# Later steps for layer 1's norms and for image 1's features, and another buffer for image 1's run weights, in a four-layer image kernel

## The chip, the cores and the metric

The kernel runs on one core of a Trainium2 chip. The metric is the device time of one execution in microseconds (us); three executions give a median. The engines are PE (TensorE, matrix products), ACT (ScalarE), DVE (VectorE), POOL (GpSimd) and SP (SyncE, which here issues DMAs).

## The reference

Four images of 64 x 64 pixels and 64 channels, float32, pass through four layers.

- Layer 0 is attention over the 4,096 pixels of an image: q, k and v are linear maps of x, and the result is `gamma * softmax(q k^T) v + x`, with a small gamma.
- Layer 1 has two halves. First: a layer norm over the channels, a pointwise map to 256 channels, a 3 x 3 depthwise convolution, the product of the two halves of the channels (a gate), a scale for each channel from the mean over all pixels (`sca`), a pointwise map to 64 channels, and `x + beta * ...`. Second: a layer norm, a pointwise map to 256, the gate, a pointwise map back to 64, and `x + gamma * ...`.
- Layer 2 is attention of the image with itself, `softmax(x x^T) x` over the pixels. Its scores are symmetric.
- Layer 3 is a non-local block with maps g, phi, theta of 32 channels, a softmax over the pixels, an output map, a batch norm over the whole batch, and a residual.

## The kernel before, in words

Everything of an image is kept in SBUF: `X[:, b]` is image b as 128 partitions (64 channels, two halves of the pixels) x 2,048 columns. Attention runs by items. An item computes a block of scores on PE into a slot of PSUM, ACT turns it into exponentials e with row sums, and PE multiplies e with the values two or so items later, into accumulator banks. PSUM is one tile PS: slots of 1,024 columns are handed out in turn by `new_ps` (two while layer 0 runs, three once image 3's last layer-0 product is out), and banks 6 and 7 accumulate.

**The order is written out by hand.** A list `items` holds layer 0 of images 0 to 3 (32 items each), then layer 2 of image 0 (100 items; I call the n-th score step of that layer row n), then layer 2 of image b with layer 3 of image b - 1, and so on. Beside it run two lanes of Python generators: `conv` (layer 1, added at item 32b + 34, so that layer 1 of image 3 begins with layer 2 of image 0) and `misc` (loads, projections, `features2`, and others). Each item advances the lanes by some nominal microseconds, and a generator's `yield us` says how far its next piece lies behind. The numbers in the yields are distances in that count, not times of the chip. The instruction order of PE, ACT, DVE and POOL is the order of recording; the order of SP's DMA queue is left to the scheduler.

**norm (L1159 to L1191)**, used twice in layer 1 of each image. Two Squares of x on ACT (L1164); after the first yield the sums on PE (L1170: four matmuls on x, four on the squares, which sum over the channels by the constant `jsel`); the variance (L1175 on ACT, L1176 on DVE); Ln and Exp on ACT (L1178, L1179); eight DMAs on SP that broadcast the result to all partitions (L1183); after a yield of 11.0 two multiplications by x on DVE (L1191).

**layer1 (L1194 to L1297).** The first norm writes y; pointwise products L1205; ACT writes them into the padded image `pad` (L1222); nine taps for each of 4 x 2 blocks (L1236 on ACT for image 3, L1240 on DVE), the gate with its sums on DVE (L1251), their total `ytot` (L1257), then the small product with `sca` on PE (L1260) and the scaled weights pw2s on DVE (L1262, L1264), and the products with them (L1269) and the residual (L1274 on ACT, L1276 on DVE). The second norm writes z; then for each of four blocks two products L1205, ACT's t (L1288), DVE's u (L1290), a product L1294 and a residual (L1295, L1297).

**features2 (L1301 to L1314)** makes the keys `ko` of layer 2 for an image: four transposes on PE (L1309), each followed by a copy on DVE and one on ACT (L1312) and a DMA on SP for each (L1313).

**Layer 2.** Scores L1387, exponentials L1392, products L1448. Because scores are symmetric, some blocks of e are used a second time, mirrored: DVE transposes them (L1405, tile `turned`), and a run of 64 small matmuls (L1473) multiplies them with the run weights `xr`, a regrouped copy of the image that 16 DMAs for each h make on SP (L1364). A run's result and an accumulator's are added to `A` by DVE (L1486, L1488, L1462; an accumulator of image 0 partly by a copy on ACT, L1459).

**Layer 0 around it.** Scores L1095, exponentials L1100, products L1121; the last products of an image are added to X, quarter by quarter, with gamma (L1133).

**Buffers that matter.** The pool "xn" has one buffer: y, z, xr of images 1 to 3, and a DMA sum of layer 3 live in it one after another. The pool "pad" has one: the padded image, and later `wy` of images 0 and 1 (layer 3's output before its batch norm). xr of image 0 has a buffer of another pool. A tile that takes over a buffer waits for the last reader of the one before.

Lines of this text and of the profile are those of the kernel before; in the changed kernel those behind L1356 are three higher.

Of the kernel before, what the change touches and what calls it, by code (L numbers as in the profile page):

```python
# [8 lines left out]
F32 = mybir.dt.float32  # L9
# [682 lines left out]
def fast_path(ctx: ExitStack, tc: tile.TileContext, a: dict, out: bass.AP, bad):  # L692
    nc = tc.nc
    B, H, W, C = a["x"].shape
# [9 lines left out]
    xn = ctx.enter_context(tc.tile_pool(name="xn", bufs=1))  # L704
# [21 lines left out]
    def new_ps():  # L726
        if turn_of["banks"]:
            if turn_of["bank"] % turn_of["banks"] == turn_of["banks"] - 1:
                turn_of["bank"] += 1
            k = new_bank(), new_bank()  # L730
            return PS[:, 512 * k[0] : 512 * k[0] + 1024]
        s = turn_of["slots"][turn_of["ps"] % len(turn_of["slots"])]
        turn_of["ps"] += 1
        return PS[:, bass.ts(s, 1024)]

    def piece():
        if turn_of["banks"]:
            return PS[:, bass.ts(new_bank(), 512)]
        return new_ps()[:, 0:512]
# [8 lines left out]
    def new_e(name="e"):  # L748
        return ep.tile([128, 2048], F32, tag="e", name=name)

    def new_t(name="t"):
        return tp.tile([128, 1024], F32, tag="t", name=name)

    def new_big(name):
        return big.tile([128, 4096], F32, tag="big", name=name)

    def new_pad(name="pad"):
        return big.tile([128, 66 * PW + 2], F32, tag="pad", name=name, bufs=1)
# [233 lines left out]
    def at(i, fn):  # L992
        due.setdefault(i, []).append(fn)
# [162 lines left out]
            items.append((lambda t=t: item(t), 0.0))  # L1156


    def norm(x, y):  # L1159


        sq = [new_t("sq"), new_t("sq")]
        for i in range(2):
            act(sq[i], x[:, bass.ts(i, 1024)], AF.Square)  # L1164
        yield 4.5
        ps = new_ps()
        for i, src in enumerate(((x, x), (sq[0], sq[1]))):
            for j in range(4):
                c = 512 * j if i == 0 else 512 * (j % 2)
                mm(  # L1170
                    ps[32 * j : 32 * j + 32, bass.ts(i, 512)], jsel, src[j // 2][:, c : c + 512],
                    start=True, stop=True,
                )
        t = new_t()
        act(t[:, 0:512], ps[:, 0:512], AF.Square)  # L1175
        stt(t[:, 0:512], t[:, 0:512], -1.0, ps[:, 512:1024], ALU.mult, ALU.add)  # L1176
        yield 4.0
        act(t[:, 0:512], t[:, 0:512], AF.Ln, bias=eps1)  # L1178
        act(t[:, 512:1024], t[:, 0:512], AF.Exp, scale=-0.5)  # L1179
        yield 3.0  # L1180
        for j in range(4):
            for h in range(2):
                nc.sync.dma_start(  # L1183
                    out=y[64 * h : 64 * h + 64, bass.ts(j, 512)],
                    in_=t[32 * j + 16 * h : 32 * j + 16 * h + 16, 512:1024]
                    .unsqueeze(1).to_broadcast([16, 4, 512]),
                )
        yield 11.0
        for jp in range(2):
            cols = bass.ts(jp, 1024)  # L1190
            nc.vector.tensor_mul(y[:, cols], y[:, cols], x[:, cols])  # L1191
            yield 1.8
# [6 lines left out]
    def layer1(b):  # L1199
        x = X[:, b]  # L1200
# [8 lines left out]
                    )  # L1209

        y = xn.tile([128, 2048], F32, tag="xn", name="xn")
        yield from norm(x, y)
        yg = new_big("yg")
        yw = yg.rearrange("c (s q p h) -> c p q s h", s=2, p=2, h=H)
        ysum = sm.tile([128, 8], F32, tag="ysum", name="ysum")
# [39 lines left out]
                    yield 1.8  # L1255
        ytot = sm.tile([128, 1], F32, tag="ytot", name="ytot")
        nc.vector.tensor_reduce(ytot, ysum, AX.X, ALU.add)  # L1257
        yield 12.0 if b == B - 1 else 7.0
        ps = new_ps()
        mm(ps[:, 0:1], sca, ytot, start=True, stop=True)  # L1260
        ch = sm.tile([128, 1], F32, tag="ch", name="ch")
# [15 lines left out]
            yield 3.0  # L1277
        z = xn.tile([128, 2048], F32, tag="xn", name="xn")
        far = 1.2 if b == B - 1 else 1.0
        for us in norm(x, z):  # L1280
            yield far * us
        for j in range(4):
            t, u = new_t(), new_t("u")
# [18 lines left out]
    def features2(b):  # L1302
        x = X[:, b]
        im[b].ko = ko = new_big("ko")
        kv = ko[:, 0:N].rearrange("p (a e n) -> p a e n", e=2, n=128)
        for g in range(4):
            ps = piece()
            for i in range(4):
                nc.tensor.transpose(ps[:, bass.ts(i, 128)], x[:, bass.ts(4 * g + i, 128)], ident)  # L1309
            for e, copy in enumerate((nc.vector.tensor_copy, nc.scalar.copy)):  # L1310
                own, other = slice(64 * e, 64 * e + 64), slice(64 - 64 * e, 128 - 64 * e)
                copy(kv[own, bass.ts(g, 4), e, :], ps[own, :].rearrange("p (a n) -> p a n", n=128))  # L1312
                nc.sync.dma_start(out=kv[other, bass.ts(g, 4), e, :], in_=kv[own, bass.ts(g, 4), e, :])  # L1313
            yield 3.5  # L1314

    SIDES = [[(7, (h + 1) % 7), ((h + 2) % 7, (h + 3) % 7)] for h in range(7)]
    FULL = [(7, [7])] + [(h, [h] + SIDES[h]) for h in range(6)] + [(6, SIDES[6] + [6])]
# [6 lines left out]
    def layer2(b, when_free=None):  # L1324


        x, m, first = X[:, b], im[b], len(items)
# [20 lines left out]
        st = {"e": {}, "T": {}, "esum": {}}  # L1348
# [8 lines left out]

        def weights(h):
            if "xr" not in st:
                st["xr"] = new_e("xr") if b == 0 else xn.tile([128, 2048], F32, tag="xn", name="xn")  # L1360
            for q in range(4):
                for k in range(4):
                    c = 1024 * (h % 2) + 256 * k
                    nc.sync.dma_start(  # L1364
                        out=st["xr"][32 * q : 32 * q + 32, c : c + 256],
                        in_=x[32 * k : 32 * k + 32, 256 * h : 256 * h + 256],
                    )
# [157 lines left out]
    def close2(b):  # L1525
        x, m = X[:, b], im[b]
        ps, tot, n = piece(), sums2[:, b, :], 4 * max(m.mirrored) + 4
        cs = m.cs.rearrange("p (j k) -> p j k", k=4)
        for k in range(4):
            mm(ps[32 * k : 32 * k + 32, 0:n], sel4, cs[:, 0:n, k], start=True, stop=True)  # L1530
        g = 0
        while g < 8:
            k = g
            while k < 8 and m.count[k] == m.count[g]:
                k += 1
            nc.vector.tensor_reduce(
                tot[:, 4 * g : 4 * k],
                m.zs[:, m.first[g] : m.first[g] + 4 * m.count[g] * (k - g)]
                .rearrange("p (t k) -> p t k", k=m.count[g]), AX.X, ALU.add,
            )  # L1540
            g = k
        nc.vector.tensor_add(tot[:, 0:n], ps[:, 0:n], tot[:, 0:n])
        rz = sm.tile([128, 32], F32, tag="rz2", name="rz2")
        nc.vector.reciprocal(rz, tot)
        yield
        for i in range(4):
            ps = new_ps()
            for j in range(8):
                c = 1024 * i + 128 * j
                nc.tensor.transpose(ps[:, bass.ts(j, 128)], m.A[:, c : c + 128], ident)  # L1550
            blocks_ = ps.rearrange("p (j n) -> p j n", n=128)
            nc.vector.tensor_mul(
                blocks_, blocks_, rz[:, bass.ts(i, 8)].unsqueeze(2).to_broadcast([128, 8, 128])
            )
            xs = x[:, bass.ts(i, 512)].rearrange("p (j h) -> p j h", h=H)
            for o in range(2):
                nc.vector.tensor_add(xs, ps.rearrange("p (j o h) -> p j o h", j=8, o=2)[:, :, o, :], xs)  # L1557
            yield
# [48 lines left out]
    def keys3(b):  # L1607
        m = im[b]
        m.ph = new_big("ph")
        keys = m.ph.rearrange("p (s n) -> p s n", s=2)  # L1610
        for j in range(4):
            for k in range(4):
                nc.sync.dma_start(
                    out=keys[32 * k : 32 * k + 32, :, bass.ts(j, 512)],
                    in_=m.own[32 * j : 32 * j + 32, :, :],
                )
# [185 lines left out]
    conv_from, misc_from, misc_to = {}, {}, {}  # L1802
    for b in range(B):
# [3 lines left out]
        if b + 1 < B:  # L1807
            gens = [load_x(i) for i in range(1, B)] if b == 0 else []
            misc_from[32 * b + 16] = gens + [project0(b + 1)]
        conv_from[32 * b + 34] = layer1(b)  # L1810
    misc_from[112] = [features2(0)]
    for b in range(B):
        misc_to[len(items)] = True
        f = len(items)
        if b == 0:
            layer2(b)
            misc_from[f + 82] = [features2(b + 1)]
        else:
            layer2(b, lambda b=b: keys3(b - 1))
            turns = close2(b - 1)  # L1820
            for i in (10, 13, 22, 32, 42) if b == 1 else (8, 12, 22, 32, 42):
                at(f + i, lambda turns=turns: next(turns))
            misc_from[f + 46] = [open3(b - 1)]
            f = len(items)
            misc_to[f] = True
            layer3(b - 1)
            if b + 1 < B:
                turns = features2(b + 1)
                for i in (4, 7, 10, 13):
                    between3[f + i] = 2, lambda turns=turns: next(turns)  # L1830
    f = len(items)
# [220 lines left out]
```

## Time and profile before

| | |
|---|---|
| median of three executions | 2459.12 us (2457.01, 2459.12, 2463.22) |
| profiled execution, whole | 2458.65 us |
| its span, first to last instruction | 2456.9 us |
| mean granted clock of PE | 0.997 |
| PE busy, idle in the span | 2412.4 us, 44.5 us |
| DVE, ACT, POOL busy | 1467.3, 1651.4, 533.0 us |
| layer 1 of image 3, from its first sums to the last residual | about 1025 to 1280 us |
| layer 2 of image 0 in PE's order | from about 1017 us on |

How to read it: a line of the timeline is the start, the duration, the engine, the source line, the operation, the tile written and those read, the shapes and how many instructions are run together; in brackets stands the idle time before and what ended it. A line of the waits is the waiting engine, tile and line, what it waited for, and then the sum in us, how often, and the longest. In a table of windows each engine has its busy time and its count, and the last three numbers are the granted clock as a share of full speed, the DMA engines' share, and GB/s.

### The profile page before, as it was taken

Reading aid. Unit: us, or ns where it says so; the run is one execution under the profiler, and the core shown is the slowest. Engines: PE = TensorE matmul, PEld = TensorE weight load, DVE = VectorE, ACT = ScalarE, POOL = GpSimd, SP = SyncE. Lnnn points to the kernel's source line nnn. Section 1 sums busy time; section 2 is a strip of 40 time slices with the busy share of each in tenths; the row PEclk is TensorE's granted clock in tenths of the full one; section 3 lists DMA queues with packets and bytes.
Section 4 is the critical chain, followed back from the end, with each engine's and each line's share of the span. In section 5 each row is a group of like instructions: output and inputs, shape, how many; then the busy total and the mean of one; then the engine's idle time right before and its main releaser. Section 6 shows DMA issues by size and latency. Waiting matters only on the chain.

```text
span 2456.9 us, 63395 instructions
## 1 busy us (share of the span) xinstructions
PE 2412.4 (98%) x27381; PEld 927.5 (38%) x27381; DVE 1467.3 (60%) x1784; ACT 1651.4 (67%) x3144; POOL 533.0 (22%) x383
## 2 busy tenths in 40 slices
PE   9999999999999999999899999999999999999998
PEld 3343453336433633344334442144431344421113
DVE  2010377227822773278656668876668866678886
ACT  4666766676666666668654459954479744579996
POOL 2000000000000000010136551255631365622110
PEclk9999999999999999999999999999999999999999
DMA  3000000000000000250530026610075300286554
GB/s 80 1 18 1 19 1 18 18 19 1 18 18 18 2 19 18 55 119 2 123 81 23 19 66 134 139 27 23 16 151 118 78 20 20 71 170 141 120 117 117
DMA packets 67668, 136.39 MB, mean 56 GB/s; under 512 B 13004, under 2 KB 34229, under 8 KB 67381
## 3 DMA queue, kind: packets, MB, share of 16 engines
q0 software_dynamic: 24320, 86.55, 17.4%
q1 hardware_dynamic: 42309, 43.85, 7.8%
q8 instruction: 217, 3.56, 0.6%
q10 hardware_dynamic: 752, 1.85, 0.2%
q14 instruction: 70, 0.57, 0.1%
HBM read 4.80 MB, written 4.19 MB: 4 GB/s over the span
## 4 chain that ended last, share of the span: by engine, by line
PE 85%; DVE 8%; ACT 4%; issue 1%; SPq 1%; DMA 0%; DVEq 0%; ACTq 0%
PE PS L1121 18%; PE PS L1095 18%; PE PS L1448 9%; PE PS L1387 9%; PE PS L1635 9%; PE PS L1696 8%; PE PS L1473 7%; DVE tg L1687 2%; PE PS L1205 2%; ACT e L1646 2%; DVE y L1240 2%; ACT e L1100 1%; PE PS L1170 1%; ACT e L1392 1%; DVE X L1557 1%
## 5 line engine op out<-in xcount | busy, mean ns | idle before, releaser
L1100 ACT ACTIVATE e<-PS 128x1024 f32<-128x1024 f32 x512 | 524.2, 1024 | 331.3 <-PE PS L1095 298.4
L1392 ACT ACTIVATE e<-PS 128x512 f32<-128x512 f32 x632 | 371.5, 595 | 350.6 <-PE PS L1387 329.9
L1121 PE MATMUL PS<-e,vq 64*64 64x512 f32 x4096 | 577.3, 592 | 0.0
L1095 PE MATMUL PS<-X,q 64*64 64x512 f32 x4096 | 574.5, 590 | 1.8 <-DVE X L979 1.7
L1646 ACT ACTIVATE e<-PS 128x512 f32<-128x512 f32 (+2 forms) x588 | 500.2, 921 | 59.3 <-PE PS L1635 38.6
L1687 DVE TENSOR_TENSOR tg<-tg,e 128x2048 f32<-128x2048 f32 x172 | 393.8, 2290 | 42.8 <-ACT e L1646 31.4
L1387 PE MATMUL PS<-ko 64*64 64x512 f32 x2528 | 346.3, 596 | 1.3 <-DVE A L1488 0.7
L1448 PE MATMUL PS<-e,X 64*64 64x512 f32 x2528 | 340.7, 593 | 1.4 <-ACT own L1459 0.8
L1240 DVE SCALAR_TENSOR_TENSOR y<-pad,vec,y 128x1024 f32<-128x1024 f32 x240 | 307.9, 1283 | 14.3 <-ACT y L1236 7.0
L1427 POOL TENSOR_TENSOR esum<-esum,e 128x1024 f32<-128x1024 f32 x126 | 299.3, 2376 | 49.0 <-ACT e L1392 42.0
L1405 DVE STREAM_TRANSPOSE turned<-e 128x1024 f32<-128x1024 f32 x196 | 240.9, 1238 | 107.5 <-ACT e L1392 107.5
L1635 PE MATMUL PS<-tg,ph 32*64 32x512 f32 x4096 | 294.9, 612 | 1.7 <-ACT e L1646 0.8
L1095 PEld LDWEIGHTS PS<-X,q 64*64 64x64 f32 x4096 | 184.1, 133 | 258.8 <-issue 178.4
L1121 PEld LDWEIGHTS PS<-e,vq 64*64 64x64 f32 x4096 | 184.2, 133 | 251.9 <-issue 158.6
L1421 POOL DMA_DIRECT2D esum<-e x28 | 22.0, 786 | 1178.1 <-ACT e L1392 1081.5
L1696 PE MATMUL PS<-e,tg 128*32 128x512 f32 x2048 | 272.5, 604 | 0.0
L1108 DVE TENSOR_REDUCE sums<-zs 128x1 f32<-128x4 f32 x128 | 19.6, 153 | 260.0 <-ACT e L1100 259.8
L1448 PEld LDWEIGHTS PS<-e,X 64*64 64x64 f32 x2528 | 104.1, 133 | 171.8 <-issue 146.7
L1473 PE MATMUL PS<-turned,xn 32*64 32x256 f32 x5376 | 163.2, 377 | 4.0 <-DVE X L1557 3.5
L1668 POOL DMA_DIRECT2D xn<-e x116 | 101.3, 903 | 293.9 <-ACT e L1646 201.0
L1387 PEld LDWEIGHTS PS<-ko 64*64 64x64 f32 x2528 | 96.4, 133 | 164.2 <-issue 135.4
L1635 PEld LDWEIGHTS PS<-tg,ph 32*64 32x64 f32 x4096 | 63.4, 129 | 222.7 <-ACT e L1646 190.2
(218 smaller groups left out, 1677.8 us busy)
## 6 DMA issues: line engine op xcount, KB each, us to landing
xn<-e POOLq DMA_DIRECT2D x132, 512.0 KB, 5.2
esum<-e POOLq DMA_DIRECT2D x28, 512.0 KB, 4.7
xn<-X SPq DMA_DIRECT2D x336, 32.0 KB
xn<-t SPq DMA_DIRECT2D x64, 128.0 KB
ph<-tg SPq DMA_DIRECT2D x64, 128.0 KB
ko<-ko SPq DMA_DIRECT2D x32, 128.0 KB
xr<-in_x_dram SPq DMA_DIRECT2D x13, 256.0 KB
q<-q SPq DMA_DIRECT2D x12, 256.0 KB
```

Source lines behind the costliest of these rows:

```text
L1095: mm(ps[64 * c : 64 * c + 64, bass.ts(r, 512)], m.q[rows_, 128 * t + 64 * c : 128 * t + 64 * c + 64], x[rows_, bass.ts(g, 512)], start=Tru ...
L1100: act(es[g // 2][:, bass.ts(g % 2, 1024)], ps, AF.Exp, bias=SHIFT0, accum_out=zs[:, g : g + 1],)
L1121: ins = mm(PS[64 * s : 64 * s + 64, 2048 + 512 * j : 2560 + 512 * j], vq[rows_, :], es[j // 2][rows_, k : k + 512], start=t == 0 and i < 2 ...
L1240: stt(y1, win, wt, y1, ALU.mult, ALU.add)
L1387: mm(ps[64 * c : 64 * c + 64, bass.ts(r, 512)], m.ko[rows_, k : k + 64], m.ko[rows_, bass.ts(h, 512)], start=True, stop=True,)
L1392: act(e[:, bass.ts(r, 512)], ps[:, bass.ts(r, 512)], AF.Exp, bias=SHIFT2, accum_out=slot(g, 2 * u + r),)
L1448: mm(st["acc"][r][64 * c : 64 * c + 64, :], xw[rows_, 4 * g + 2 * u + c, :], st["e"][n][rows_, bass.ts(c, 512)], start=n == mine[h][0], st ...
L1473: mm(slots[q // 2][64 * c : 64 * c + 64, o : o + 256], st["xr"][rows_, w : w + 64], T[rows_, bass.ts(e, 256)], start=e < 2, stop=e >= 14,)
L1635: mm(PS[64 * c : 64 * c + 64, bass.ts(banks[k], 512)], m.ph[32 * k : 32 * k + 32, 128 * mc + 64 * c : 128 * mc + 64 * c + 64], m.th[32 * k ...
L1646: act(e[:, 512 * lo : 512 * k], PS[:, 512 * banks[lo] : 512 * banks[lo] + 512 * (k - lo)], AF.Exp,)
L1687: nc.vector.tensor_add(esum, esum, e)
L1696: mm(st["y"][32 * k : 32 * k + 32, :], m.gx[:, i % 32, :], es[i][:, bass.ts(k, 512)], start=mc == 0, stop=i % 32 == 31,)
```

## The change

Three things. The pieces of the norms are recorded somewhat later: the first yield of `norm` is 5.5 in place of 4.5 (both norms, all images), and for image 3 alone the yield before the multiplications is 2.0 longer in the first norm and 4.0 x 1.2 in the second, and that behind `ytot` is 14 in place of 12. `features2` of image 1 is recorded from item 89 of layer 2 of image 0 in place of 82, with its four pieces 3.0 apart in place of 3.5 (the 3.0 and 3.5 are the same code for images 0 and 1; image 2 and 3 call it from elsewhere, item by item). The run weights xr of image 1 live in the pad's buffer.

```diff
-    def norm(x, y):
+    def norm(x, y, more):
...
             act(sq[i], x[:, bass.ts(i, 1024)], AF.Square)
-        yield 4.5
+        yield 5.5
         ps = new_ps()
...
-        yield 11.0
+        yield 11.0 + more
         for jp in range(2):
             cols = bass.ts(jp, 1024)
             nc.vector.tensor_mul(y[:, cols], y[:, cols], x[:, cols])
...
-        yield from norm(x, y)
+        yield from norm(x, y, 2.0 if b == B - 1 else 0.0)
...
         nc.vector.tensor_reduce(ytot, ysum, AX.X, ALU.add)
-        yield 12.0 if b == B - 1 else 7.0
+        yield 14.0 if b == B - 1 else 7.0
...
-        for us in norm(x, z):
+        for us in norm(x, z, 4.0 if b == B - 1 else 0.0):
             yield far * us
...
-            yield 3.5
+            yield 3.0
...
-                st["xr"] = new_e("xr") if b == 0 else xn.tile([128, 2048], F32, tag="xn", name="xn")
+                st["xr"] = (
+                    new_e("xr") if b == 0 else new_pad("xr") if b == 1
+                    else xn.tile([128, 2048], F32, tag="xn", name="xn")
+                )
...
-            misc_from[f + 82] = [features2(b + 1)]
+            misc_from[f + 89] = [features2(b + 1)]
```

## The prediction

> **What bounds the kernel now.** I read the page's totals first, then the chain that ended last, the waits of TensorE (PE), and then the timeline around each wait, together with the granted clock.
>
> ```profile
> span 2456.9 us, 63395 instructions
> ...
> PE 2412.4 (98%) x27381; PEld 927.5 (38%) x27381; DVE 1467.3 (60%) x1784; ACT 1651.4 (67%) x3144; POOL 533.0 (22%) x383
> ...
> PE 85%; DVE 8%; ACT 4%; issue 1%; SPq 1%; DMA 0%; DVEq 0%; ACTq 0%
> ```
>
> PE is busy 98% and carries 85% of the chain. The change adds and removes no matmul, so it can only move PE's idle time (44.5 us) and whatever slows PE down. PE's waits, largest first:
>
> ```profile
> PE PS L1205 <- issue: 4.4, 1, 4.4
> ...
> PE PS L1170 <- ACT e L1100: 2.1, 3, 0.7
> ...
> PE PS L1260 <- DVE ytot L1257: 1.8, 1, 1.8
> PE PS L1205 <- ACT e L1392: 1.7, 1, 1.7
> ...
> PE PS L1309 <- ACT ko L1312: 0.9, 1, 0.9
> ```
>
> Columns: total us, times, longest. All five lie in lines that the change reschedules. Matmuls are pipelined, so a group's duration overlaps the next: a group shown as x8 costs 0.86 from start to start. I take a gap from there, not from the bracket. The 4.4 stands for 4.57 (the last group would end at 1222.57, the next starts at 1227.14), the first-norm 1.7 for 2.76, the 1.8 for 1.94.
>
> Three places in the timeline, with the releaser in brackets:
>
> ```profile
> 269.58 1.70 PE L1170 MATMUL PS<-sq,jsel 128*32 128x512 f32 x8
> ...
> 450.21 1.06 PE L1170 MATMUL PS<-X,jsel 128*32 128x512 f32 x8 [0.69 <-ACT e L1100]
> ...
> 447.16 1.99 ACT L1164 ACTIVATE sq<-X 128x1024 f32<-128x1024 f32 x2
> ...
> 1046.77 2.06 PE L1205 MATMUL PS<-xn,pw 64*64 64x512 f32 x16 [1.75 <-ACT e L1392]
> ...
> 1227.14 1.98 PE L1205 MATMUL PS<-xn,pw 64*64 64x512 f32 x8 [4.39 <-issue]
> 1228.87 3.66 PE L1448 MATMUL PS<-e,X 64*64 64x512 f32 x16
> ...
> 1225.87 2.31 DVE L1191 TENSOR_TENSOR xn<-xn,X 128x1024 f32<-128x1024 f32 x2
> ```
>
> The 1227.14 group takes 1.98 where its like take 1.04, and the next 3.66 where 1.90 is usual. Two-microsecond windows show why (PE busy, PEld, DVE, ACT, POOL, then the granted clock):
>
> ```profile
> 1224.00:1226.00 2.00, 0.00 (x0) 0.00 (x0) 2.00 (x3) 0.71 (x4) 1.35 (x3) 0.92 0.80 179
> 1226.00:1228.00 2.00, 0.86 (x4) 0.33 (x8) 2.00 (x2) 0.00 (x0) 0.00 (x0) 0.50 0.97 297
> ...
> 1230.00:1232.00 2.00, 2.00 (x12) 0.55 (x9) 0.00 (x0) 0.30 (x1) 0.00 (x0) 0.50 0.00 0
> 1232.00:1234.00 2.00, 2.00 (x20) 0.74 (x16) 0.00 (x0) 0.46 (x1) 0.00 (x0) 0.87 0.00 0
> ```
>
> The clock fell to half at about 1225.7, 3.1 us into the gap, and came back at about 1232.5. PE worked 5.4 us at half speed (1227.14 to 1232.5) and lost 2.7. So the wait in front of the second norm's product costs 4.57 + 2.7 = 7.3, and it is the only place before the tail where the clock dips: the 2.76 gap at 1044 left it at 1.00.
>
> **The change, part by part.** The profiled execution took 2458.65 us (span 2456.9 and 1.75 around it); the median of the runs is 2459.12, 0.5 above it. The sum is made against 2458.65.
>
> (a) Norm's first yield, 4.5 to 5.5, images 0 to 2, no bytes or instructions added. In the changed order the sums L1170 stand one score and one product later on PE (about 1.7 us), while the two Squares (1.99) stay where they were on ACT. Second norms: three gaps of 0.76 (PE free at 449.45, start 450.21), because the exp that frees the PS slot ran behind the Squares. One step later that exp has ended (450.05 and 450.96 for the two slots). First norms: L1170's second group takes until 271.21 instead of 270.56, hidden wait 0.65, three alike. Gain 3 x 0.76 + 3 x 0.65 = **4.2**. L1205 moves by a step at most, and the exps beside it give the slack. If the wait passes to the next score instead, the gain is 0: bounds 0 to 4.2, and I take 4.2 because the exps' ends in the row above precede the new starts.
>
> (b) The same yield, image 3, first norm. L1170 moves from layer 2's score 4 to score 5, and thereby behind two of the last gamma updates L1133, which write X: it now waits for DVE. Chain: exps of that score end at 1028.7 on ACT (behind the Squares, 1026.39, and the 1.15 of the exps before), the transpose L1405 takes 1.2, two L1133 1.37: 1031.4. PE is free at 1027.5, so a new wait of 3.9. The next two updates are late as well, behind a transpose that waits for exps of a score issued after L1170: first product L1448 then waits 1.55. Added 5.45. Removed: 1.76 in rows 7 and 8 (the score group 1031.99 and the product 1034.50: four steps of 2.57 from 1031.09 would reach 1041.39, not 1043.15) and the 2.76 before L1205, which moves a row later, behind a 3.64 run of L1473 that covers it. Net 5.45 - 4.52 = **+0.9**. Bounds: -3.0 (the wait for L1133 shrinks to nothing) and +0.9 plus a clock dip of 2.7.
>
> (c) ytot, 12 to 14. L1260 moves from row 75 to 78, so its 1.94 goes. But in row 76 the products L1448 need the accumulator that the A add L1462 frees (1178.82, 0.69), and DVE runs that add behind the same chain of taps and L1257: PE stops there until about 1180.5, a row step later than before, 2.5 us. After it, pw2s (L1262, L1264) stands behind two transposes, and L1269 waits about 1.2. Net 2.5 + 1.2 - 1.94 = **+1.8**; bounds -1.9 and +2.7.
>
> (d) Second norm of image 3 (4.0 x 1.2 more), features2 seven steps later and 3.0 apart. L1170 moves from row 82 to 85, the pw3 products L1205 from row 90 to 94, the four transposes L1309 from rows 83 to 88 to rows 90 to 95. Removed: 4.57, the 2.7 of the clock, and 0.94 (L1309): 8.2. New, by the same chaining: the third L1309 waits for the ACT copy behind the muls, 1.0; L1205 waits for the mul (the broadcasts end about 1226, the mul stands behind a transpose), 1.3; three slot waits, 1.15 together; and in row 95 the run L1473 needs the slot that u (L1290, 1.28) frees, 2.1. Sum 5.5, each below 3.1, so no dip. Net **-2.7**; bounds -8.2 and +1 (the adds A<-own took 2.36 at 1222.41, 1.41 elsewhere).
>
> (e) Queues. On SP image 1's first 32 run loads (L1364, 0.69 each by the 22.00 at 1013.61, 1.04 by the 33.42 of a later 32 at 1068.80) now stand ahead of the second norm's 8 broadcasts (11.07), and these ahead of all 8 ko DMAs. The loads wait for the pad's last reader, about 1179: they end by 1202 or 1213, and Exp has the broadcasts' source at about 1215. Cost **0**, and the ko DMAs have rows 95 to 100 before the first score needs them. Cover gone, each microsecond costs one. POOL's queue gets nothing new.
>
> (f) xr of image 1 in the pad's home: **0**. Before, its loads started at 1271.37, behind z's last reader, and the first run product at 1284.03 had no wait. With z read four rows later this would have been late; the pad takes that away. wy of images 0 and 1 takes the pad only after the last run, so it waits for nothing new.
>
> Sum: -4.2 + 0.9 + 1.8 - 2.7 = -4.2, so 2454.5.
>
> [...]
>
> **Rivals.** R1: the new waits of (b) to (d) hardly form, since rows drift; only L1170's half remains. Then (a) 4.2, (b) 1.0 gained, (c) 0.5, (d) 6: 11.7, 2447. For it: each new wait hangs on one or two transposes' place. Against: the order on DVE is fixed.
>
> R2, the waits only change their name: (a) passes to the next score, (c) and (d) stay, 2457 to 2460. For it: PE's 44.5 idle follow from ACT and DVE, whose work is unchanged.
>
> R3, slower: the loads on SP hold the broadcasts up. They decide from the point where they end after about 1216 (L1205 at 1229, less 11.07 and 2 for landing). At 1.38 each, what a broadcast took, 32 from 1180 end at 1224: 8 late, and a gap that long brings back the dip, 2.7. -4.2 + 10.7 gives 2465; with the pad freed some microseconds later 2470. For it: the chain of SP waits is long (one load waited 43.1). Against: the 0.69 and 1.04 rows.
>
> R4, slower: L1170's 3.9 halves the clock in (b), and the drift adds a microsecond to each of (c) and (d): 2454.5 + 3 + 2 = 2459.5 to 2461.
>
> **How the numbers follow.** Forecast 0.40 (its own range 2450 to 2458), R1 0.27 (2444 to 2450), R2 0.14, R3 0.11, R4 0.08. Range 2444 to 2464: it leaves out most of R3 and R1's tail. About 0.3% (7.4 us) is what a measurement of this kernel can tell from no change; the three runs spread over 6.2. Faster means below 2451.7: R1 whole and a quarter of the forecast, 0.37. Slower means above 2466.5: half of R3, and a little of what I have not seen, 0.12. Same 0.51.
>
> **What would show it.** Right: L1170 at 1.04 in all six norms of images 0 to 2, and no wait on L1100; a wait of L1170 on DVE X L1133 near 1031; L1260 without a wait and an L1448 waiting for DVE near 1180; no 4.4 wait and the clock at 1.00 from 1224 to 1234. Wrong: the clock at 0.50 after the L1170 wait; SP still issuing L1364 (after: L1367) beyond 1216; waits on ACT e L1100 moved to L1095.

## The result, and the profile after

The changed kernel takes 2466.31 us (median of 8, 2465.44 to 2469.57), the kernel before 2459.0 (median of 8, 2455.02 to 2463.22). The ratio is 1.0032 with the 95% interval 1.0021 to 1.0043: 7.3 us slower, where 4.2 us faster was forecast, and above the range. The profiled execution has a span of 2464.8.

The page's totals and chain after:

```profile
span 2464.8 us, 63383 instructions
...
PE 2417.4 (98%) x27381; PEld 927.8 (38%) x27381; DVE 1466.6 (60%) x1784; ACT 1648.2 (67%) x3144; POOL 531.7 (22%) x383
...
PE 83%; DVE 10%; ACT 5%; issue 1%; SPq 1%; DMA 1%; DVEq 0%; ACTq 0%
```

PE executes the same 27,381 matmuls and is busy 5.0 us longer (2412.4 before): the same work ran more slowly for a while. DVE's share of the chain went from 8 to 10%. PE's waits, from the top:

```profile
PE PS L1451 <- DVE A L1465: 4.9, 2, 3.7
PE PS L1170 <- DVE X L1133: 3.9, 1, 3.9
...
PE PS L1170 <- ACT e L1100: 2.3, 3, 0.8
...
PE PS L1476 <- DVE u L1290: 1.3, 1, 1.3
PE PS L1205 <- issue: 1.2, 1, 1.2
...
PE PS L1269 <- ACT e L1395: 0.9, 1, 0.9
```

The 4.4 in front of the second norm's product has become 1.2, the wait for ytot is gone, and the 1.75 in front of the first norm's products is down to 0.46. The first two lines are new. Two-microsecond windows around them (columns as before; the granted clock is the third number from the end):

```profile
1028.00:1030.00 2.00, 0.00 (x0) 0.00 (x0) 1.96 (x3) 0.00 (x0) 0.00 (x0) 0.73 0.23 59
1032.00:1034.00 2.00, 2.00 (x15) 0.32 (x10) 0.00 (x0) 0.17 (x1) 0.00 (x0) 0.50 0.13 33
...
1184.00:1186.00 2.00, 0.00 (x0) 0.00 (x0) 1.93 (x7) 0.00 (x0) 0.55 (x1) 0.98 0.85 332
1188.00:1190.00 2.00, 2.00 (x12) 0.49 (x8) 0.86 (x1) 0.00 (x0) 0.00 (x0) 0.50 0.10 23
```

The clock halved towards the end of each of the two waits, from about 1028.9 to 1035.7 and from 1185.9 to 1192.7, so that PE worked 5.6 us (from 1030.11) and 6.1 us (from 1186.64) at half speed and lost about 2.8 and 3.0 (the ends by the clock of 0.57 in 1034 to 1036 and of 0.81 in 1192 to 1194). The kernel before had one such dip, after the 4.4 wait; that one is gone (1.00 from 1220 to 1232).

The timeline after, of PE and then of DVE:

```profile
271.91 1.07 PE L1170 MATMUL PS<-X,jsel 128*32 128x512 f32 x8 [0.83 <-ACT e L1100]
...
1030.11 1.94 PE L1170 MATMUL PS<-X,jsel 128*32 128x512 f32 x8 [3.94 <-DVE X L1133]
...
1186.64 2.83 PE L1451 MATMUL PS<-e,X 64*64 64x512 f32 x11 [3.70 <-DVE A L1465]
...
1068.45 2.61 DVE L1240 SCALAR_TENSOR_TENSOR y<-pad,vec,y 128x1024 f32<-128x1024 f32 x2 [5.03 <-ACT y L1236]
...
1185.81 0.16 DVE L1257 TENSOR_REDUCE ytot<-ysum 128x1 f32<-128x8 f32 x1
1185.89 0.69 DVE L1465 TENSOR_TENSOR A<-PS,A 128x512 f32<-128x512 f32 x1
```

The wait at 1030 is the one that step (b) forecast, with the length forecast. The lines to compare on DVE are two of the kernel before:

```profile
1062.12 6.53 DVE L1240 SCALAR_TENSOR_TENSOR y<-pad,vec,y 128x1024 f32<-128x1024 f32 x5
...
1178.82 0.69 DVE L1462 TENSOR_TENSOR A<-PS,A 128x512 f32<-128x512 f32 x1
```

From the first tap on DVE to the A add are 116.7 us before and 117.4 after. The chain got only 0.7 longer; it began 6.3 us later and ended 7.1 later, while PE was 4.0 later at the score of row 75 (table below). So PE stood waiting at its end.

Where the 7.9 of the profiled executions (2464.8 - 2456.9) come from, by start times of PE groups with equal work ahead of them:

| PE group | before | after | later by | new in this stretch |
|---|---|---|---|---|
| first score of layer 2 | 1017.65 | 1016.23 | -1.4 | layer 0: -1.4 |
| second run L1473 (row 17) | 1065.53 | 1068.48 | 3.0 | (b): +4.4 |
| third run | 1086.72 | 1091.71 | 5.0 | a first wait for an A add (1.2): +2.0 |
| score of row 75 | 1176.25 | 1180.20 | 4.0 | -1.0 |
| run in row 81, with one L1269 (1.0) still owed | 1195.33 | 1205.09 | 10.8 | (c): +6.8 |
| image 1's second run, and everything behind it | 1293.93 | 1301.86 | 7.9 | (d): -2.8 |

### The profile page after: what moved, and what is told of

Read it like the earlier page. It is cut to its first block, busy times and chain, and to the rows that moved or that the text cites. A ratio compares the mean times of both kernels' runs of the same rounds, so it can differ in the third digit from the quotient of the medians.

```text
span 2464.8 us, 63383 instructions
## 1 busy us (share of the span) xinstructions
PE 2417.4 (98%) x27381; PEld 927.8 (38%) x27381; DVE 1466.6 (60%) x1784; ACT 1648.2 (67%) x3144; POOL 531.7 (22%) x383
## 4 chain that ended last, share of the span: by engine, by line
PE 83%; DVE 10%; ACT 5%; issue 1%; SPq 1%; DMA 1%; DVEq 0%; ACTq 0%
PE PS L1121 18%; PE PS L1095 17%; PE PS L1638 8%; PE PS L1390 8%; PE PS L1451 8%; PE PS L1699 8%; PE PS L1476 7%; DVE tg L1690 3%; DVE y L1240 2%; PE PS L1205 2%; ACT e L1649 2%; ACT e L1395 1%; DVE X L1560 1%; PE PS L1170 1%; PE PS L1553 1%
## 5 line engine op out<-in xcount | busy, mean ns | idle before, releaser
L1121 PE MATMUL PS<-e,vq 64*64 64x512 f32 x4096 | 573.2, 592 | 0.0
L1390 PE MATMUL PS<-ko 64*64 64x512 f32 x2528 | 352.1, 599 | 0.9 <-DVE A L1491 0.7
L1451 PE MATMUL PS<-e,X 64*64 64x512 f32 x2528 | 347.2, 594 | 5.8 <-DVE A L1465 4.9
L1240 DVE SCALAR_TENSOR_TENSOR y<-pad,vec,y 128x1024 f32<-128x1024 f32 x240 | 309.8, 1291 | 18.5 <-ACT y L1236 11.3
L1121 PEld LDWEIGHTS PS<-e,vq 64*64 64x64 f32 x4096 | 182.2, 133 | 255.1 <-issue 160.3
L1451 PEld LDWEIGHTS PS<-e,X 64*64 64x64 f32 x2528 | 107.9, 134 | 176.5 <-issue 148.0
L1395 ACT ACTIVATION_READ_ACCUMULATOR e<-PS 128x1 f32 x632 | 127.6, 202 | 0.0
```

The source lines that it names most:

```text
L1121: ins = mm(PS[64 * s : 64 * s + 64, 2048 + 512 * j : 2560 + 512 * j], vq[rows_, :], es[j // 2][rows_, k : k + 512], start=t == 0 and i < 2 ...
L1240: stt(y1, win, wt, y1, ALU.mult, ALU.add)
L1390: mm(ps[64 * c : 64 * c + 64, bass.ts(r, 512)], m.ko[rows_, k : k + 64], m.ko[rows_, bass.ts(h, 512)], start=True, stop=True,)
L1395: act(e[:, bass.ts(r, 512)], ps[:, bass.ts(r, 512)], AF.Exp, bias=SHIFT2, accum_out=slot(g, 2 * u + r),)
L1451: mm(st["acc"][r][64 * c : 64 * c + 64, :], xw[rows_, 4 * g + 2 * u + c, :], st["e"][n][rows_, bass.ts(c, 512)], start=n == mine[h][0], st ...
```

## The experiments

Two theories for the loss. C: the two new waits are paid twice, once as idle time and once in the slow clock after them. And behind that the question what makes the waits: S, image 3's first sums behind the gamma updates; P, its first pointwise products behind the run of row 11; or the yield behind ytot. All times below are medians, with the ratio to the kernel before on the same chip and its 95% interval. The kernel before took 2459.0 to 2460.5 on these chips, so a difference between medians of different chips is good to about 1.5 us at best. For the edits, `norm` has its first yield as a parameter `first` (5.5 wherever nothing else is said):

```diff
-    def norm(x, y, more):
+    def norm(x, y, more, first):
...
-        yield 5.5
+        yield first
```

**Fill the two waits (`warm`, `warm2`).** The changed kernel with repeated matmuls:

```diff
-        for i, src in enumerate(((x, x), (sq[0], sq[1]))):
+        for i, src in ((1, sq),) * warm + ((0, (x, x)), (1, sq)):   # warm = 3 in image 3's first norm, else 0
...
+            for _ in range(14 if b == 0 and n == mine[6][0] else 0):   # 3 in warm2
+                mm(
+                    st["acc"][0][0:64, :], xw[0:64, 4 * g + 2 * u, :], st["e"][n][0:64, 0:512],
+                    start=True, stop=True,
+                )
             for r, c in quads:
```

> The changed kernel, with matmuls added that fill most of its two long waits and change no result: three more passes of the sums of the squares (0.88 us each) ahead of image 3's first L1170, and 14 repeats of the first product (0.215 each) ahead of the one that waits for DVE's A add near 1186. No instruction that anything waits for moves. Theory C (the two waits are paid twice, because the granted clock halves after them): the clock stays at 1.00 through 1025-1040 and 1180-1195, and the time falls by about 3 us for the first dip and 2.7 for the second: 2460 to 2461.5. Theory O (the order alone, through its waits, makes the loss; a slower PE there is slack): within 1 us of the changed kernel's 2466.3. If the repeats only delay PE, 2467 or more.

Measured: 2467.39 (1.0030, 1.0021 to 1.0040). The mean granted clock of the profiled run was 0.999, for 0.996 in the changed kernel, but a repeat took about 0.8 us in place of 0.215, so that the 14 took about 11 us in place of 3: far past the A add, which they were to end ahead of. The price of a repeat was wrong, and the run says nothing on what the second dip costs.

> As the first filled kernel (three more passes of the squares' sums ahead of image 3's first L1170), but 3 repeats of the product ahead of the wait for the A add near 1186 instead of 14: in the trace of the first one a lone repeat took about 0.8 us and not 0.215 (it uses a quarter of the array, and only four different ones run side by side), so that the 14 ran past the wait. No instruction that anything waits for moves. Theory C (the halved clock is paid in full): no dip in either place and 2460 to 2461.5, that is 5 to 6 us below the changed kernel. Theory O (the slower PE is slack): 2465 to 2467. Between: the first dip alone counts, about 2463.5, because the second stretch of PE work is again waiting for something.

Measured: 2462.25 (1.0015, 1.0006 to 1.0024), 4.1 below the changed kernel, with more matmuls in it. The windows of this kernel at the two places:

```profile
1026.00:1030.00 4.00, 3.06 (x28) 0.73 (x32) 2.54 (x3) 1.00 (x4) 0.00 (x0) 1.00 0.22 55
1030.00:1036.00 6.00, 5.44 (x46) 1.45 (x42) 2.77 (x4) 3.94 (x10) 1.12 (x2) 1.00 0.25 85
...
1184.00:1190.00 6.00, 6.00 (x56) 2.02 (x48) 3.62 (x4) 2.53 (x8) 1.24 (x2) 1.00 0.34 80
```

The clock stays at 1.00, and the time falls, less than theory C said (5 to 6). So the two new dips cost about 4 us; the intervals of the two ratios allow about 1 to 8, so this run does not tell theory C in full from the case in between (2463.5). It takes the slow clock away and leaves what ends the waits as it is. The rest of the 7.3 is the balance of the waits that came and those that went, the old dip of 2.7 among them.

**Sums and products, one at a time.** Three kernels complete a square with the changed one. Each is the changed kernel with other numbers in one line:

```diff
-        yield from norm(x, y, 2.0 if b == B - 1 else 0.0)
+        yield from norm(x, y, 4.0 if b == B - 1 else 0.0, 3.5 if b == B - 1 else 5.5)   # sums4_pw12
+        yield from norm(x, y, 1.0 if b == B - 1 else 0.0, 3.5 if b == B - 1 else 5.5)   # sums4_pw11
+        yield from norm(x, y, 0.0, 4.5 if b == B - 1 else 5.5)                          # sums5_pw11
```

> The changed kernel with one thing moved back: image 3's first sums L1170 in score row 4 again (ahead of the gamma updates), the first pointwise products L1205 left in rows 12 to 15. Theory S (the wait of L1170 on the gamma updates, with its dip, is what starts the loss, and all that follows on DVE shifts with it): first tap about 5 us earlier than in the changed kernel (1063.5 for 1068.5), time 2460 to 2462. Theory P (L1205 behind the run L1476 delays the taps, DVE has no slack from there to ytot, and that is most of the loss): first tap at most 3 us earlier, time 2464 to 2466.

> The changed kernel with image 3's first sums in row 4 and the first pointwise products from row 11 on (one per row, where the kernel before had two in row 11). Both theories S and P: no dip near 1030, first tap at 1062 to 1064, PE's wait for the A add near 1180 no longer than 2.5 us, and so no dip there: 2455 to 2458, below the kernel before because the second norm's 4.4 us wait stays away. If the ytot wait keeps 3 us or more, its cause is step (c), not the late taps, and the time stays above 2460.

> The changed kernel with image 3's first pointwise products from row 11 on, ahead of the run, its first sums left in row 5. It completes a square with the changed kernel (sums 5, products 12: 2466.3), sums 4 and products 12 (2460.8), sums 4 and products 11 (2456.9). Theory: the two moves cost DVE's chain their own lateness each and add up: 2466.3 - 3.9 = 2462.4. Rival: the wait of L1170 hides the later products or the other way round; then it is 2460.8 or lower, or 2465 or higher.

Measured:

| image 3's first sums | first products from row 12 | from row 11 |
|---|---|---|
| in row 5, behind L1133 | 2466.31 (the changed kernel) | 2462.76 (1.0016, 1.0007 to 1.0025) |
| in row 4 | 2460.80 (1.0000, 0.9991 to 1.0009) | 2456.91 (0.9987, 0.9978 to 0.9996) |

By the medians the sums' row is worth 5.5 to 5.9 and the products' row 3.5 to 3.9, and the sum of the two fits the changed kernel, as expected. With both moved back the whole loss is gone. With sums4_pw12 DVE's taps start at 1061.84 and ytot's total stands at 1179.20; with sums4_pw11 1059.95 and 1175.44; with sums5_pw11 1063.50 and 1179.01; in the changed kernel 1068.45 and 1185.81. The distance is 115.5 to 117.4 in all of them. Both theories S and P hold, each with its share. But they cost PE in different places, as its wait at the end of the chain shows (sums4_pw12, sums4_pw11, sums5_pw11):

```profile
1180.03 2.83 PE L1451 MATMUL PS<-e,X 64*64 64x512 f32 x11 [3.69 <-DVE A L1465]
```

```profile
1176.27 1.51 PE L1451 MATMUL PS<-e,X 64*64 64x512 f32 x11 [1.71 <-DVE A L1465]
...
1228.44 1.99 PE L1205 MATMUL PS<-xn,pw 64*64 64x512 f32 x8 [4.58 <-issue]
```

```profile
1179.83 1.82 PE L1451 MATMUL PS<-e,X 64*64 64x512 f32 x11 [1.71 <-DVE A L1465]
...
1233.57 1.99 PE L1205 MATMUL PS<-xn,pw 64*64 64x512 f32 x8 [4.58 <-issue]
```

With the products from row 12 the wait for the A add is 3.70 and 3.69, whichever row the sums have; with row 11 it is 1.71 both times. So the sums' wait on the gamma updates holds PE and DVE up together, and it is the later products that let DVE fall behind PE. The wait of 1.2 at an earlier A add goes the same way: 1.20 and 1.19 with row 12, none with row 11. One expectation failed: in both kernels with row 11 all that follows in layer 1 stands a row earlier, the second norm's products in row 93 for 94, and their wait of 4.6 is back with its dip of the clock (the group behind it takes 1.99 in both; in sums5_pw11 the clock is 0.71 in 1230 to 1235 and 0.61 in 1235 to 1240). So what the products' row is worth is net of that. And row 11 is filled by one of the products that the kernel before had two of there, so the run of 3.64 no longer stands ahead of all of them.

**The yield behind ytot.**

```diff
-        yield 14.0 if b == B - 1 else 7.0
+        yield 12.0 if b == B - 1 else 7.0
```

> The changed kernel with 12 in place of 14 behind ytot. L1260 moves one row up, to 77, and stays behind the products that wait for the A add, so that wait (3.7) and its dip stay: 2465 to 2467 if the A add behind DVE's chain is what PE waits for whatever the yield says. The pw3 products come a row earlier too, which may bring the second norm's 4.6 wait back: then 2468 to 2470. If step (c) made the loss, 2461 to 2463.

Measured: 2468.92 (1.0033, 1.0021 to 1.0045). The wait for the A add is 3.7 as in the changed kernel, and the second norm's products, a row earlier, wait 4.6 again. So the yield that step (c) is about does not make the wait for the A add, and putting it back gains nothing; what it is worth by itself cannot be told here, since the other wait came with it.

**Single parts on the kernel before.** `d_only` has the second norm's longer distances in image 3 (5.5 and 4.0 x 1.2), features2 from item 89 on and 3.0 apart, and xr in the pad's home; `d_no_pad` the same without the last; `a_only4` the 5.5 of images 0 to 2 alone, with image 3's sums in row 4 and its products from row 11 (`first` 3.5 and `more` 1.0 in its first norm, 4.5 and 0.0 in its second).

> The kernel before with steps (d) to (f) alone: the second norm of image 3 with the longer distances, features2 of image 1 from item 89 on and 3.0 apart, xr of image 1 in the pad's home; all else as before. By the prediction's step (d): the 4.4 us wait and its clock dip go, waits of about 5.5 come: 2.7 less than before, 2456. Rival: the waits that come take as much as those that go, 2458.5 to 2460. If it is above 2462, the loads ahead of the broadcasts on SP matter after all.

> Steps (d) and (e) without (f): the kernel before with the longer second norm and the later features, but xr of image 1 behind z in the xn buffer. By the prediction's (f) the loads are late then: z's last reader comes two to four rows later than before (1276 to 1280 for 1271), 32 loads take 22 us or more, the first run stands near 1283: 5 to 12 us above the 2454.7 with the pad, 2460 to 2467. If it stays at 2455, the pad is worth nothing.

> The kernel before with step (a) alone: 5.5 in both norms of images 0 to 2; image 3's first sums held in row 4 and its first pointwise products in row 11 (one per row). By the prediction's (a): 4.2 less. By the trace of the changed kernel (the second norms' three waits of 0.76 go, the first norms' hidden 0.65 becomes a visible 0.8): about 2 less in layer 0, and the 2.8 wait at image 3's first products may go as well; together 2455 to 2458. Rival (waits are only renamed): 2459 to 2460.

Measured: d_only 2454.73 (0.9972, 0.9961 to 0.9983), d_no_pad 2458.80 (0.9994, 0.9985 to 1.0003), a_only4 2451.07 (0.9972, 0.9960 to 0.9984). So the part about the second norm and the features gains 5.5 when it stands alone, more than the 2.7 of step (d). In both profiles PE gains 4.8 on the kernel before between the run of row 81 and image 1's first run. Without the pad 4.1 of the 5.5 are lost, a little less than expected; in the profile of d_no_pad the late loads take back 2.9 at image 1's first run. The first run on image 1, in d_no_pad and then in d_only:

```profile
1280.16 5.08 PE L1476 MATMUL PS<-turned,xn 32*64 32x256 f32 x122 [1.26 <-DMA xn<-X]
```

```profile
1282.61 3.71 PE L1476 MATMUL PS<-turned,xr 32*64 32x256 f32 x128
```

a_only4 gains 8. In its profile layer 0 holds 1.5 of that (first score of layer 2 at 1016.15), image 3's first products 1.9, and the second norm most: PE is 3.8 ahead of the kernel before at the run of row 81 and 10.0 ahead at the run behind the second norm's products. These stand in row 91 for 90, wait 1.8 for 4.4, and the clock holds:

```profile
1222.22 1.21 PE L1205 MATMUL PS<-xn,pw 64*64 64x512 f32 x8 [1.83 <-ACT e L1395]
...
1220.00:1225.00 5.00, 3.17 (x32) 2.04 (x32) 5.00 (x5) 2.38 (x5) 1.43 (x2) 1.00 0.98 288
1225.00:1230.00 5.00, 5.00 (x47) 2.71 (x39) 4.03 (x5) 3.07 (x10) 0.87 (x1) 1.00 1.07 201
```

At image 1's first run, whose loads are late, 2.0 go back.

The 1.9 at the first products goes with a cause that nobody had in mind. SP starts the 32 loads of image 0's xr at 1011.26 in place of 1013.61, and the first norm's broadcasts behind them at 1033.01 in place of 1035.78; the products in row 11 then find y ready. All ten kernels with 5.5 in the first norms of images 0 to 2 start these loads between 1010.5 and 1011.9, all four with 4.5 between 1013.4 and 1013.9. In the kernel before the first load waits for a product of layer 0 (L1121) and then for ACT's t of image 2 (L1288), in a_only4 for the product alone; what moves these is not shown. Nor does the loads' start set the wait by itself: with 4.5 and the same recorded order up to there, the kernel before, d_only and d_no_pad wait 1.75, 3.54 and 0.94 at image 3's first products in their profiles. Their loads start within 0.3 us of each other, and the first multiplication that waits for the broadcasts starts at 1045.44, 1047.31 and 1044.43.

**Put together.** `bestA` is the changed kernel with 4.5 in the first norms of images 0 to 2, image 3's sums in row 4 and products from row 11, and `more` 6.0 in its second norm. `a4_pad` is a_only4 with xr of image 1 in the pad's home, and `a4_pad_m` has `more` 2.5 in image 3's second norm besides:

```diff
-        for us in norm(x, z, 0.0 if b == B - 1 else 0.0, 4.5 if b == B - 1 else 5.5):
+        for us in norm(x, z, 2.5 if b == B - 1 else 0.0, 4.5 if b == B - 1 else 5.5):
```

> A version put together from what the runs showed: first norms of images 0 to 2 as before (4.5), second norms 5.5; image 3's first sums in row 4, its first products one per row from row 11; ytot 14; the second norm's multiplication 6.0 later in place of 4.0, so that its products stand in row 94 as in the changed kernel; features2 and xr as in the changed kernel. Expected: no dip of the clock at all before the tail, the waits left on PE in layer 2 of image 0 about 1.7 (A add), 1.0 (L1269), 1.2 to 2 (second norm), 1.3 (run's slot): 2452 to 2454. If the second norm's wait comes back with its dip: 2456.

> The fastest so far (step (a) alone with image 3's first sums in row 4 and its first products from row 11, 2451.1) plus xr of image 1 in the pad's home, nothing else. In the trace of that kernel the first run on image 1 took 5.44 us at 1274.65 where a run takes 3.71, its loads having started only at 1265.0, behind z's last reader. Expected: that run at 3.7, about 1.7 us less, 2449 to 2450. Rival: the 32 loads now stand ahead of the second norm's broadcasts on SP and delay them; then the wait of the second norm's products (1.8) grows past 3 us, the clock dips, and the time is 2452 or more.

> As the one before, and the second norm's multiplication 2.5 later, so that its products start in row 92 in place of 91. The wait of about 2 us there goes or falls under 0.5, with no other row of layer 1's first half changed: 1.5 less than the one before, 2447 to 2449. If the time stays, the wait has moved to the products' own slots.

Measured: bestA 2456.69 (0.9992, 0.9983 to 1.0001), a miss: with 4.5 in the first norms of images 0 to 2 the loads on SP start at 1013.90 again, image 3's first products wait 3.5, and the clock falls behind that wait (0.89 in 1045 to 1050, 0.76 in 1050 to 1055). Layer 0 gains nothing either: the second norms have 5.5, yet their three waits of 0.69 (by the brackets) are there as in the kernel before. So 5.5 in the second norms alone does not move their sums. a4_pad 2450.75 (0.9955, 0.9942 to 0.9969): the run is down to 3.71, yet the time is that of a_only4 within what can be told, and this profile has a dip of the clock near 1178 that a_only4's does not have (0.69 for 1.00 in 1175 to 1180). The dip may not be in every execution: the three that took 2450.75 to 2451.12 have a mean clock of 0.998, the two that took 2447.74 and 2448.55 have 0.999. a4_pad_m 2447.82 (0.9946, 0.9933 to 0.9960): 18.5 below the changed kernel and 11 to 13 below the one before. The second norm's wait went from 1.83 to 1.25 only, not under 0.5. It is the best version found here, and it has two of the change's three ideas: 5.5 in images 0 to 2, and the pad.

## Why the prediction was wrong, point by point

(a) Forecast -4.2, measured -1.4 (0.7 to 2.5 between the profiles with 5.5 in the first norms and those with 4.5). The second norms' three waits of 0.76 went, as the exps' ends said. The first norms' hidden 0.65 did not: one step later L1170 takes the PS slot whose exp runs behind the Squares, and waits 0.83 (the line at 271.91), 0.76 and 0.76. The step took the slot of one kind of norm for that of the other. What it missed altogether is SP: with the same yield the xr loads start 2.3 earlier.

(b) Forecast +0.9, measured +4.4. The wait (3.9) was right, and so was its cause. The dip behind it was named and put into a bound and into R4 at 0.08; it came, and cost about 2.8 (5.6 us of work at half speed). The second wait of 1.55 came as 0.56. Of the 4.52 that the step took off, 2.76 stand for the wait in front of L1205; by the step's own way of counting that wait is 1.9, since the last scores ahead of it start at 1044.43 and cost 0.43. And the claim that the products' move behind the run is covered by the run was wrong: PE had other work, but the taps on DVE start from these products. With the L1170 wait, its dip and the later products together the taps began 6.3 later.

(c) Forecast +1.8, measured +6.8. This is the step that failed worst. It named the right wait (L1451 for the A add behind ytot), sized it at 2.5 and dated its end near 1180.5, because it moved DVE's chain by a row step. The chain is 116.7 us long with DVE busy for 104.6 of them, and it moved by all that (b) had delayed its start: PE's wait ended at 1186.6. It was 3.7 long, and the clock halved in it, which cost about 3.0 (6.1 us of work at half speed) and which the step did not count. By the square the length of 3.7 comes from the products' row, the part of (b) that was called covered, and not from the L1170 wait, which made PE later as well. The +2.0 at the third run is the same lateness at an earlier A add.

(d) Forecast -2.7, measured -2.8 in place. The 4.4 wait and its dip went; waits of 0.9, 1.2, 0.2 and 1.3 came (by the brackets; from start to start about 5), each where the step had put it. Its "below 3.1, so no dip" held there, but is no rule: in a4_pad_m the clock halved 0.8 us behind a wait of 1.94 (0.87 in 1176 to 1178, then 0.50; last section). That the part gains 5.5 alone and that after_ytot12 brings the 4.6 wait back show how narrow its place is: one row.

(e), (f) Forecast 0, and no wait of PE is put down to these queues. SP issued the last of the 32 loads at 1210.2 and the first broadcast at 1222.48, as the source came; R3 did not happen. The pad is needed beside (d): d_no_pad.

Of the rivals R4 had part of the mechanism and at most a third of the size, 2459.5 to 2461, because it counted one dip where there were two, and a microsecond for the drift in (c). Its 3 for a dip was the author's estimate, beside the 2.7 measured behind the 4.4 wait; the two dips cost 2.8 and 3.0. R1 and R2 fell. The sum's fault in one sentence: it priced the products' move where PE felt it first, at the products, and not at the end of the DVE chain that began there, and it left the dips in the two new waits, 2.8 and 3.0, out of the sum.

## What to carry to other kernels

Where two engines are both nearly full, ask of every moved instruction not only whether its own engine has other work, but when the longest chain on the other engine starts from it, and price the delay at that chain's end. A wait on PE can have a second price in the clock: behind the waits of 3.94 and 3.70 it was about 2.8 and 3.0 us here. A few matmuls without use in the waits took that price away (clock 1.00 at both places in warm2, 4.1 us less). And a distance written in a recording order can move what stands in the DMA queue too, and every later piece of the same lane by a row: so several of the single changes here brought an old wait back.

## What the runs showed of the hardware

In these runs the length of a wait alone did not decide whether the clock fell. The wait in front of L1170 was followed by half clock in the changed kernel (3.94; 0.50 in 1032 to 1034) and by full clock in sums5_pw11 (3.95; 1.00):

```profile
1029.32 1.06 PE L1170 MATMUL PS<-X,jsel 128*32 128x512 f32 x8 [3.95 <-DVE X L1133]
...
1028.00:1030.00 2.00, 0.68 (x8) 0.34 (x12) 1.17 (x2) 0.00 (x0) 0.00 (x0) 1.00 0.20 49
1030.00:1032.00 2.00, 2.00 (x20) 0.52 (x16) 0.04 (x1) 0.60 (x1) 0.00 (x0) 1.00 0.22 56
```

And the wait of 1.9 for ytot, the same in both, was followed by full clock in a_only4 (1.95; 1.00) and by half clock in a4_pad_m (1.94; 0.50), two lines each:

```profile
1176.22 0.35 PE L1260 MATMUL PS<-ytot,sca 128*128 128x1 f32 x2 [1.95 <-DVE ytot L1257]
...
1178.00:1180.00 2.00, 2.00 (x24) 1.28 (x20) 1.31 (x3) 0.37 (x1) 0.00 (x0) 1.00 0.50 190
```

```profile
1176.69 0.35 PE L1260 MATMUL PS<-ytot,sca 128*128 128x1 f32 x2 [1.94 <-DVE ytot L1257]
...
1178.00:1180.00 2.00, 2.00 (x16) 1.13 (x12) 1.79 (x4) 0.00 (x0) 0.00 (x0) 0.50 0.95 314
```

A shorter wait of 1.71 in sums5_pw11 (the line at 1179.83 above) was followed by half clock too (0.73 in 1180 to 1182, then 0.50), while the gap of 2.76 in the kernel before left the clock at 1.00:

```profile
1182.00:1184.00 2.00, 2.00 (x10) 0.26 (x3) 0.05 (x1) 0.00 (x0) 0.00 (x0) 0.50 0.52 164
```

So these runs give no length of wait from which on the clock falls, and what decides is not shown.

A 64 x 64 product that was repeated alone cost 0.86 us (three, shown as x6, in 2.58 from 1178.81 to 1181.39 in warm2), as much as the four products of one group on their four different quarters together (x8 in 0.86 from start to start: 1176.24 to 1177.10 in the same run).
